# Runs of 32 in the loads of w1 and w2, zeros set by VectorE, and another order of the first rows, copies and fillers

## The chip, the cores and the metric

The kernel runs on 1 core of one Trainium2 chip. The metric is the device time of one launch in microseconds. Before the change it was 1922.45 us (median of three runs, 1921.44 to 1922.81).

## The reference

Inputs: x (8 batches of 1024 rows of 128), proj_q and proj_o (8 heads of 128x128), proj_k and proj_v (128x128), w1 (8 experts, 128x512), w2 (8 experts, 512x128), all float32. In short:

```python
xn = layernorm(x)                                   # over the last 128
Q = einsum('bnd,hdk->bhnk', xn, proj_q); K = xn @ proj_k; V = xn @ proj_v
weights = softmax(einsum('bhnk,bmk->bhnm', Q, K))
Y = einsum('bhnv,hdv->bnd', einsum('bhnm,bmv->bhnv', weights, V), proj_o)
mid = einsum('amh,ehn->aemn', xn, w1)
out = x + Y + einsum('aemn,enh->amh', mid, w2)
```

Keys and values are shared by the heads, and there is no nonlinearity between w1 and w2.

## The kernel before

**What is computed.** Per head the query and key projections are multiplied into one matrix (`wqk_product`), and the value and output projections into another (`wvo_product`), so that the logits are (xn wqk) xn^T. w1 and w2 are multiplied and summed over experts and hidden units into a single 128x128 matrix `wf` (`ffn_weights`). A unit u is one batch and head, 64 in all. A row i is one block of 128 queries against all 1024 keys, 8 to a unit and 512 in all. The product of weights and values uses a scheme with seven products instead of eight (`product`, with sums and differences of blocks made by GpSimd in `sum_early` and `sums_late`, and of values at the end of `values`).

**A row.** `logits(i)` is two halves of matmuls (`logits_half`, eight 512-wide matmuls together: each float32 product is two instructions, for two halves of the array). `exponents(i)` takes the row maximum on VectorE (`nmax`) and the exponential on ScalarE, which also gives the row's sum. `divide(i)` takes the reciprocal on VectorE (`rinv`) and multiplies on ScalarE. `weights_t(i - 1)` turns the weights of the row before in blocks of 32x32 on VectorE, and after each fourth row `move_blocks` moves the blocks between partitions with 16 DMAs on SyncE's queue (SP), which completes the transposition. Twelve rows later (`LAG`) the products of the unit follow, `PAIRS` of them to a row; a pair is four 512-wide matmuls. The last four rows use `LAST_PAIRS`, and turn their weights on TensorE (`weights_t_pe`).

**What sets the order.** It is written out by hand: each engine runs its instructions in the order of the program text. Two PSUM buffers (tag `sc`) serve the logits in turn, so the logits of row i wait until the exponents of row i-2 (or, with a large query product between, of row i-1) have been read. Four more banks (`bank`, tags `acc0` to `acc3`) serve the small products of the start in turn. A bank is free when its copy to SBUF is done.

**The start.** SP loads x's first batch in four pieces, then the projections, w1, w2 and the next batch's rows. Statistics (`stats_pair`), normalization (`norm_pair`) and transposition (`xn_t_pair`) go by pairs of 128-row chunks. `keep_clock` puts filler matmuls on zeros (`idle`, written to PSUM tile `pidle`) between them; GpSimd sets the zeros. Then the table `early` names which preparations go behind the logits of which row: the other wqk products, the queries, the transposes of proj_o (`wo_part`), the wvo products, the first values and the ffn products. `W1` names the rows after which VectorE turns a quarter of w1.

**w1 and w2.** w1 is held as `w1s`, two halves of four experts. Hidden units are spread over partitions so that 32x32 turns on VectorE bring them onto partitions. Before, a half is one DMA in which a partition receives 8 KB in one piece, and both sides of the turn (`turn_w1`, L224) step through memory in strides (16 elements read, 4 written). w2 has a partition order to match.

Of the kernel before, what the change touches and what calls it, by code (L numbers as in the profile page):

```python
# [9 lines left out]
F32 = mybir.dt.float32  # L10
AF = mybir.ActivationFunctionType
ALU = mybir.AluOpType
AX = mybir.AxisListType
# [4 lines left out]
def kernel(  # L18
# [76 lines left out]
    def slot(name):  # L95
        return ps_sc.tile([P, S], F32, tag="sc", name=name)
# [69 lines left out]


    for e in range(2):
        w1_e = w1[ts(e, NQ)].rearrange("r (j c) n -> (r j) (c n)", c=NQ)
        nc.sync.dma_start(w1s[:, e].rearrange("p c n -> p (c n)"), w1_e)  # L170
    for e in range(2):
        w2_e = w2[ts(e, NQ)].rearrange("r (q b) h -> (r q) b h", q=Q)
        nc.sync.dma_start(w2s[e], w2_e)
    load_rows(1)

    idle = late.tile([P, GS], F32, tag="diff", name="idle")
    nc.gpsimd.memset(idle, 0.0)
    ident = const.tile([P, P], F32, tag="ident", name="ident")
    make_identity(nc, ident)
    eps = const.tile([P, 1], F32, tag="eps", name="eps")  # L180
# [40 lines left out]
    def turn_w1(k):  # L221

        e, half = divmod(k, 2)
        nc.vector.transpose(  # L224
            w1T[:, ts(k, NB)].rearrange("p b (j c) -> p c b j", c=NQ),
            w1s[:, e].rearrange("p c (q b) -> p c b q", q=Q)[:, :, ts(half, NB)],
        )

    def ffn_weights(k):
# [57 lines left out]
    def xn_t_pair(k, copy):  # L287

        if k == 0:
            xnTs[0] = batch.tile([P, S], F32, tag="xnT", name="xnT_0")  # L290
        pt = bank(f"pxn_0_{k}")
        for c in range(2):
            nc.tensor.transpose(pt[:, ts(c, P)], xns[0][:, 2 * k + c, :], ident)
        copy(xnTs[0][:, ts(k, 2 * P)], pt[:, : 2 * P])

    def queries(u, first=0, last=S, copy=nc.scalar.copy):
        b, h = divmod(u, H)
        if first == 0:
            qTs[u] = work.tile([P, S], F32, tag="qT", name=f"qT_{u}")
        n = last - first  # L300
        pq = slot(f"pq_{u}") if n == S else bank(f"pq_{u}_{first}")
        for c in range(0, n, GS):
            w = min(GS, n - c)
            both_halves(pq[:, c : c + w], wqk[:, h, :], xnTs[b][:, first + c : first + c + w])
        copy(qTs[u][:, first:last], pq[:, :n])  # L305

    def values(s, c, copy=nc.scalar.copy):

        b, k = divmod(s, 2)
        if c == 0:  # L310
            vfs[s] = batch.tile([P, GN, 7, HC, HP], F32, tag="vf", name=f"vf_{s}")
        vf = vfs[s]
        if s == 0:
            pv = [bank(f"pv_{s}_{c}_{g}") for g in range(2)]
        else:
            both = slot(f"pv_{s}_{c}")
            pv = [both[:, ts(g, GS)] for g in range(2)]
        for g in range(2):
            both_halves(pv[g], xnTs[b][:, ts(c + g * HC, P)], wvo[:, ts(k, GN), :])
        v1, v2 = (t.rearrange("p (h j x) -> p h j x", h=GN, j=2) for t in pv)  # L320
        b11, b21, b22, t4, t1, t2, t3 = (vf[:, :, f, c] for f in range(7))
        b12 = t1
        nc.scalar.copy(vf[:, :, 0:5:4, c], v1)  # L323
        copy(vf[:, :, 1:3, c], v2)
        nc.gpsimd.tensor_sub(t3, b22, b12)  # L325
        nc.gpsimd.tensor_sub(t1, b12, b11)  # L326
        nc.gpsimd.tensor_sub(t2, b22, t1)
        nc.gpsimd.tensor_sub(t4, b21, t2)

# [4 lines left out]
    def logits_half(i, g):  # L336
        u, n = divmod(i, NB)
        if g == 0:
            pls[i] = slot(f"pl_{i}")
        both_halves(  # L340
            pls[i][:, ts(g, GS)], qTs[u][:, ts(n, P)], xnTs[u // H][:, ts(g, GS)]
        )

    def exponents(i):
        pl = pls.pop(i)
        nmax = small.tile([P, 1], F32, tag="nmax", name=f"nmax_{i}")
        nc.vector.reduce_max(nmax, pl, AX.X, negate=True)  # L347
        sums[i] = small.tile([P, 1], F32, tag="sums", name=f"sums_{i}")
        if i == NS - GN:
            spare.append(scratch("vf", VF, batch))  # L350
        if i < NS - GN:
            es[i] = work.tile([P, S], F32, tag="e", name=f"e_{i}")
        else:
            es[i] = spare[0][:, ts(i + GN - NS, S)]
        nc.scalar.activation(es[i], pl, AF.Exp, bias=nmax, accum_out=sums[i])  # L355

    def logits(i):
        logits_half(i, 0)
        logits_half(i, 1)
        exponents(i)  # L360

    def divide(i):
# [288 lines left out]
    def copy_wqv(first, last, copy):  # L651
        copy(wqvT[:, first:last], pwqs.pop(first)[:, : last - first])
# [6 lines left out]
    def keep_clock(*widths):  # L659

        for n in widths:
            nc.tensor.matmul(
                pidle[:, :n], lhsT=idle[:, :P], rhs=idle[:, :n], start=True, stop=True
            )
# [4 lines left out]
    def stats_pair(k):  # L669
        row_stats(x_0, 0, (2 * k, 2 * k + 1))  # L670

    pidle = slot("pidle")
    xns[0] = rows_tile("xn_0")
    keep_clock(GS)
    stats_pair(0)
    transposed(wkqT, [wk, wqv[:, 0]], "pwk", nc.scalar.copy)
    keep_clock(P, P, P)
    stats_pair(1)
    wqk_product(0, 1)
    keep_clock(P, P)  # L680
    norm_pair(0)
    xn_t_pair(0, nc.scalar.copy)
    keep_clock(P)
    norm_pair(1)
    xn_t_pair(1, nc.scalar.copy)
    stats_pair(2)
    queries(0, 0, P)
    stats_pair(3)
    queries(0, P, GS)
    logits_half(0, 0)  # L690
    turn_wqv(1, 5)
    norm_pair(2)
# [2 lines left out]
    xn_t_pair(3, nc.vector.tensor_copy)  # L695
    copy_wqv(1, 5, nc.scalar.copy)
    turn_wqv(5, 9)
    copy_wqv(5, 9, nc.vector.tensor_copy)
    logits_half(0, 1)
    exponents(0)  # L700

    def on_vector(task, *args):
        return lambda: task(*args, nc.vector.tensor_copy)

    early = {
        1: [on_vector(wqk_product, 1, 3), lambda: queries(0, GS, S)],
        2: [on_vector(wqk_product, 4, 4), lambda: queries(1, 0, GS)],
        3: [
            on_vector(wo_part, 0),
            lambda: wo_part(1, nc.scalar.copy),  # L710
            lambda: queries(1, GS, S),
        ],
        4: [lambda: wvo_product(0), on_vector(wvo_product, 1)],
        5: [on_vector(values, 0, 0)],
        6: [on_vector(values, 0, 1)],
        7: [on_vector(values, 0, 2)],
        9: [lambda: values(0, 3)],
        10: [lambda: ffn_weights(0), lambda: ffn_weights(1)],
        11: [lambda: ffn_weights(2), lambda: ffn_weights(3)],
    }  # L720
    W1 = {0: [0], 9: [1], 10: [2, 3]}

    PAIRS = (2, 2, 1, 2)
    LAST_PAIRS = (2, 1, 1, 1)
    COLLECT = {0: [0], 2: [1], 3: [2, 3], 4: [4], 6: [5], 7: [6, 7, 8], 8: [9], 10: [10], 11: [11]}

    FIRST_ROWS = 4
# [20 lines left out]

    for i in range(NS):
        m = i % GN  # L750
        if i > 0:
            logits(i)
        for task in early.get(i, ()):
            task()
        if 0 <= i - 1 < NS - GN:
            weights_t(i - 1)
        divide(i)
        for k in W1.get(i, ()):
            turn_w1(k)


        v, n = divmod(i - LAG, NB)
        if n == 6 and v + 1 >= 0:
            sum_early(v + 1)


        if i >= LAG:
            run((PAIRS if i < NS - GN else LAST_PAIRS)[m] + (n == 0 and v % H == H // 2 + 1) * 2)
            if n == 0:
                sums_late(v, nc.gpsimd)  # L770
        if i % NB == 0 and i > 0 and i // NB + 1 < B * H:
            queries(i // NB + 1)
        if i % NB == GN and i >= LAG:
            s, r = divmod(i + 20, 32)
            if s < 2 * B:
                values(s, r // NB)


        if i == 8:
            load_x(0)  # L780
        if i == NS // B:
            ones_of_last_rows()
        for b in range(1, B):
            r = i - FIRST_ROWS if b == 1 else i - (b - 2) * H * NB - 44
            if r in ROWS:
                ROWS[r](b)
            r = i - 20 if b == 1 else i - (b - 1) * H * NB
            if r in (0, 4, 8, 12):
                if r == 0:
                    turn_rows(b)  # L790
                move_rows(b, r // 4)
        b, r = divmod(i - 23, H * NB)
        if r == 0 and b < B:
            row_diff(b)


        b, r = divmod(i - 69, H * NB)
        if 0 <= b:
            for n in COLLECT.get(r, ()):
                collect(b, n)  # L800
            if r in (15, 19, 23, 27):
                if r == 15:
                    turn_out(b)
                move_out(b, (r - 15) // 4)
            elif r == 36:
                finish(b)
            elif r == 39:
                store(b)
            elif r == 43:
                load_x(b + 1)  # L810
# [1 line left out]
    sum_early(B * H - 1)  # L812
    weights_t_pe(NS - 4)
    weights_t_pe(NS - 3)
    run(3)
    weights_t_pe(NS - 2)
    weights_t_pe(NS - 1)
    for j in range(2):
# [39 lines left out]
```

## Time and profile before

| | |
|---|---|
| median of three runs | 1922.45 us |
| the profiled execution | 1922.09 us, of which the span of instructions is 1920.0 us |
| TensorE (PE) busy | 1910.9 us |
| VectorE (DVE) busy | 1405.5 us |
| GpSimd (POOL) busy | 1406.6 us |
| ScalarE (ACT) busy | 1352.9 us |
| granted TensorE clock | 1.000 |
| first matmul of a product with the weights (L448) | 58.74 us |

The page of the profile counts busy time by engine, and the timeline lists instructions by their start. Matmuls are pipelined: the busy time given for a group of them reaches past the start of the next group. PEld is TensorE's loading of weights, SPq the DMA issue queue of SyncE. L103 is the line of a helper, so that the tile's name tells the matmuls apart: `pl` logits, `pq` queries, `pv` values, `pwqk` and `pwvo` products of projections, `pwf` products of w1 and w2, `pxn` transposes of rows, `pe` transposes of the last weights.

### The profile page before, as it was taken

How to read it: one execution, taken by the hardware profiler on the slowest of the kernel's cores; microseconds unless marked ns; L12 is line 12 of the kernel's file. 1: busy time of each engine (PE TensorE's matmuls, PEld its weight loads, DVE VectorE, ACT ScalarE, POOL GpSimd, SP SyncE). 2: the span in 40 equal slices, each digit the busy share in tenths (PEclk: the TensorE clock that was granted, in tenths of full speed). 3: DMA queues.
4: the chain of work that ended last, by engine and by line, in shares of the span. 5: the costliest groups of instructions: out<-in, count | busy, mean ns of one | idle time of the engine just before them, and what ended most of it. 6: DMA issues, size and time to landing. Idle time of an engine off the chain costs nothing.

```text
span 1920.0 us, 26851 instructions
## 1 busy us (share of the span) xinstructions
PE 1910.9 (100%) x9026; PEld 649.2 (34%) x9026; DVE 1405.5 (73%) x1783; ACT 1352.9 (70%) x1818; POOL 1406.6 (73%) x593
## 2 busy tenths in 40 slices
PE   9999999999999999999999999999999999999998
PEld 4433333333333333333333333333333333333333
DVE  7777778767786777777777777776778776777775
ACT  7677777777776777777777777777677766777764
POOL 2877777688676886777967778768687777677764
PEclk9999999999999999999999999999999999999999
DMA  6676676676766766677667676676767667567673
GB/s 196 145 158 145 143 155 155 148 166 148 161 144 153 172 152 144 151 159 166 143 152 158 152 172 138 155 156 146 183 139 153 148 155 171 132 141 157 153 163 90
DMA packets 140137, 293.49 MB, mean 153 GB/s; under 512 B 40928, under 2 KB 74464, under 8 KB 139488
## 3 DMA queue, kind: packets, MB, share of 16 engines
q1 hardware_dynamic: 139168, 291.39, 67.5%
q8 instruction: 72, 1.18, 0.3%
q14 instruction: 65, 0.53, 0.1%
q10 hardware_dynamic: 832, 0.39, 0.1%
HBM read 13.76 MB, written 4.19 MB: 9 GB/s over the span
## 4 chain that ended last, share of the span: by engine, by line
PE 76%; POOL 10%; SPq 5%; DVE 3%; ACT 2%; DMA 2%; issue 1%; POOLq 0%; ACTq 0%; DVEq 0%
PE pl L103 36%; PE acc L448 31%; SPq L403 5%; PE pv L103 4%; PE pq L103 4%; POOL f L426 3%; POOL g L423 3%; POOL g L424 3%; DVE nmax L347 2%; DMA g<-turned 1%; ACT e L355 1%; DVE turned L387 1%; PE acc L481 1%; ACT e L365 1%; POOL vf L326 0%
## 5 line engine op out<-in xcount | busy, mean ns | idle before, releaser
L103 PE MATMUL pl<-xnT,qT 128*64 128x512 f32 x4096 | 966.5, 592 | 1.4 <-ACT e L355 0.9
L347 DVE TENSOR_REDUCE nmax<-pl 128x1 f32<-128x1024 f32 x512 | 626.4, 1224 | 405.3 <-PE pl L103 404.6
L448 PE MATMUL acc<-g,vf 128*64 128x512 f32 x2560 | 852.2, 592 | 0.0
L355 ACT ACTIVATE e<-pl,nmax 128x1024 f32<-128x1024 f32 x508 | 565.7, 1114 | 406.1 <-DVE nmax L347 406.1
L365 ACT ACTIVATE e<-e,rinv 128x1024 f32<-128x1024 f32 x508 | 583.4, 1148 | 117.8 <-DVE rinv L364 117.6
L387 DVE STREAM_TRANSPOSE turned<-e 128x1024 f32<-128x1024 f32 x508 | 628.8, 1238 | 10.3
L103 PEld LDWEIGHTS pl<-xnT,qT 128*64 128x64 f32 x4096 | 292.9, 137 | 587.6 <-issue 536.5
L448 PE MATMUL acc<-f,vf 128*64 128x512 f32 x1016 | 487.0, 592 | 0.0
L423 POOL TENSOR_TENSOR g<-g,g 128x2048 f32<-128x2048 f32 x63 | 287.0, 4556 | 267.1 <-DMA g<-turned 135.4
L448 PEld LDWEIGHTS acc<-g,vf 128*64 128x64 f32 x2560 | 250.4, 137 | 510.8 <-issue 507.1
L418 POOL TENSOR_TENSOR f<-g 128x2048 f32<-128x2048 f32 x63 | 287.1, 4557 | 168.2 <-PE acc L448 87.0
L426 POOL TENSOR_TENSOR f<-g,g 128x2048 f32<-128x2048 f32 x63 | 287.4, 4562 | 4.9
L424 POOL TENSOR_TENSOR g<-f,g 128x2048 f32<-128x2048 f32 x63 | 286.9, 4554 | 0.3 <-PE acc L448 0.3
L448 PEld LDWEIGHTS acc<-f,vf 128*64 128x64 f32 x1016 | 139.2, 137 | 0.0
L103 PE MATMUL pq<-xnT,wqk 128*64 128x512 f32 (+1 forms) x516 | 121.5, 590 | 0.5 <-DVE wqk L214 0.5
L103 PE MATMUL pv<-wvo,xnT 128*64 128x512 f32 x512 | 120.8, 592 | 0.0
L364 DVE RECIPROCAL rinv<-sums 128x1 f32<-128x1 f32 x512 | 83.9, 164 | 47.8 <-ACT scratch_vf L355 4.0
L355 ACT ACTIVATION_READ_ACCUMULATOR e<-pl,nmax 128x1 f32 x508 | 97.4, 192 | 0.0
L325 POOL TENSOR_TENSOR vf<-vf 128x256 f32<-128x256 f32 x64 | 46.9, 732 | 36.2 <-ACT vf L323 30.9
L305 ACT COPY qT<-pq 128x1024 f32<-128x1024 f32 (+2 forms) x67 | 64.0, 955 | 0.0
L103 PEld LDWEIGHTS pv<-wvo,xnT 128*64 128x64 f32 x512 | 36.7, 137 | 73.5 <-issue 69.7
L103 PEld LDWEIGHTS pq<-xnT,wqk 128*64 128x64 f32 x516 | 36.7, 137 | 72.2 <-issue 70.7
(107 smaller groups left out, 545.1 us busy)
## 6 DMA issues: line engine op xcount, KB each, us to landing
g<-turned SPq DMA_DIRECT2D x2032, 128.0 KB, 2.4
xn<-in_L_attn_x_dram SPq DMA_DIRECT2D x7, 512.0 KB, 4.7
xnT<-xnt SPq DMA_DIRECT2D x112, 32.0 KB, 1.9
out<-yt SPq DMA_DIRECT2D x112, 32.0 KB, 1.9
x<-in_L_attn_x_dram SPq DMA_DIRECT2D x6, 512.0 KB, 4.3
out_dram<-x SPq DMA_DIRECT2D x6, 512.0 KB, 5.4
scratch_g<-in_L_ffn_w_dram SPq DMA_DIRECT2D x2, 1024.0 KB, 8.3
scratch_f<-in_L_ffn_w_dram SPq DMA_DIRECT2D x2, 1024.0 KB, 12.0
```

The lines of the kernel that those rows point to most:

```text
L103: nc.tensor.matmul(dst[r], lhsT=lhsT[:, r], rhs=rhs, start=start, stop=stop)
L347: nc.vector.reduce_max(nmax, pl, AX.X, negate=True)
L355: nc.scalar.activation(es[i], pl, AF.Exp, bias=nmax, accum_out=sums[i])
L364: nc.vector.reciprocal(rinv, sums.pop(i))
L365: nc.scalar.mul(es[i], es[i], rinv)
L387: nc.vector.transpose(turned[k].rearrange("p k c t q -> p c k t q")[:, :, :, j, :], es.pop(i).rearrange("p (c k q) -> p c k q", k=NQ, q=Q),)
L403: nc.sync.dma_start(dst[ts(d, Q), r], src[ts(r, Q), d])
L418: nc.gpsimd.tensor_add(f1s[u], key_half(g0s[u], 0), key_half(g0s[u], 1))
L423: engine.tensor_sub(x1, y1, x1)
L424: engine.tensor_sub(x2, f1s[u], y1)
L426: engine.tensor_sub(f4s[u], y2, x2)
L448: nc.tensor.matmul(accs[b, acc][ts(half, HP)], lhsT=vfs[u // GN][:, u % GN, f, c, :], rhs=w[:, :, c, :], start=(h == 0 and c == first), st ...
```

## The change

- w1: eight DMAs instead of two. Piece c of a half gives each partition 2 KB, one expert's row among 32 consecutive ones, and the source runs over 4 experts, 32 rows and 512 columns. A turn then reads and writes runs of 32 elements.
- w2: eight DMAs instead of two, one an expert, in which each of 32 partitions receives 16 pieces of 512 bytes.
- VectorE sets the zeros of the fillers. There is one 128-wide filler more ahead of the first transposes, and two fewer around the first row transposes.
- In the first rows the row maximum is an instruction of its own step (`row_max`), and the logits of row 1 go ahead of the loop. The copies of products go to ScalarE, or are deferred (`defer`) and flushed to VectorE behind the reciprocal of the row. The table of preparations, the turns of w1 and the last rows' pairs are spread otherwise.

```diff
     for e in range(2):
-        w1_e = w1[ts(e, NQ)].rearrange("r (j c) n -> (r j) (c n)", c=NQ)
-        nc.sync.dma_start(w1s[:, e].rearrange("p c n -> p (c n)"), w1_e)
+        for c in range(NQ):
+            w1_c = w1[ts(e, NQ)].rearrange("r (c j) n -> c r j n", c=NQ)[c]
+            nc.sync.dma_start(w1s[:, e, c], w1_c)
     for e in range(2):
-        w2_e = w2[ts(e, NQ)].rearrange("r (q b) h -> (r q) b h", q=Q)
-        nc.sync.dma_start(w2s[e], w2_e)
+        for r in range(NQ):
+            w2_r = w2[e * NQ + r].rearrange("(b q) h -> q b h", q=Q)
+            nc.sync.dma_start(w2s[e][ts(r, Q)], w2_r)
...
-    nc.gpsimd.memset(idle, 0.0)
+    nc.vector.memset(idle, 0.0)
...
         nc.vector.transpose(
-            w1T[:, ts(k, NB)].rearrange("p b (j c) -> p c b j", c=NQ),
-            w1s[:, e].rearrange("p c (q b) -> p c b q", q=Q)[:, :, ts(half, NB)],
+            w1T[:, ts(k, NB)].rearrange("p b (c j) -> p c b j", c=NQ),
+            w1s[:, e].rearrange("p c (b q) -> p c b q", q=Q)[:, :, ts(half, NB)],
         )
...
-        nc.gpsimd.tensor_sub(t3, b22, b12)
-        nc.gpsimd.tensor_sub(t1, b12, b11)
-        nc.gpsimd.tensor_sub(t2, b22, t1)
-        nc.gpsimd.tensor_sub(t4, b21, t2)
+        def differences(copy):
+            nc.gpsimd.tensor_sub(t3, b22, b12)
+            nc.gpsimd.tensor_sub(t1, b12, b11)
+            nc.gpsimd.tensor_sub(t2, b22, t1)
+            nc.gpsimd.tensor_sub(t4, b21, t2)
+        deferred.append(differences)
+        if copy != defer:
+            flush(copy)
...
+    nmaxs = {}
+    def row_max(i):
+        nmaxs[i] = small.tile([P, 1], F32, tag="nmax", name=f"nmax_{i}")
+        nc.vector.reduce_max(nmaxs[i], pls[i], AX.X, negate=True)
     def exponents(i):
-        pl = pls.pop(i)
-        nmax = small.tile([P, 1], F32, tag="nmax", name=f"nmax_{i}")
-        nc.vector.reduce_max(nmax, pl, AX.X, negate=True)
+        pl, nmax = pls.pop(i), nmaxs.pop(i)
...
         logits_half(i, 1)
+        row_max(i)
         exponents(i)
...
+    deferred = []
+    def defer(dst, src):
+        deferred.append(lambda copy: copy(dst, src))
+    def flush(copy):
+        while deferred:
+            deferred.pop(0)(copy)
...
-    keep_clock(GS)
+    keep_clock(GS, P)
     stats_pair(0)
     transposed(wkqT, [wk, wqv[:, 0]], "pwk", nc.scalar.copy)
     keep_clock(P, P, P)
     stats_pair(1)
     wqk_product(0, 1)
-    keep_clock(P, P)
+    keep_clock(P)
     norm_pair(0)
     xn_t_pair(0, nc.scalar.copy)
-    keep_clock(P)
     norm_pair(1)
     xn_t_pair(1, nc.scalar.copy)
+    queries(0, 0, P)
     stats_pair(2)
-    queries(0, 0, P)
+    queries(0, P, GS, defer)
     stats_pair(3)
-    queries(0, P, GS)
+    flush(nc.scalar.copy)
     logits_half(0, 0)
     turn_wqv(1, 5)
...
     turn_wqv(5, 9)
-    copy_wqv(5, 9, nc.vector.tensor_copy)
+    copy_wqv(5, 9, nc.scalar.copy)
     logits_half(0, 1)
+    row_max(0)
     exponents(0)
-
-    def on_vector(task, *args):
-        return lambda: task(*args, nc.vector.tensor_copy)
+    logits_half(1, 0)
+    logits_half(1, 1)
+    row_max(1)
     early = {
-        1: [on_vector(wqk_product, 1, 3), lambda: queries(0, GS, S)],
-        2: [on_vector(wqk_product, 4, 4), lambda: queries(1, 0, GS)],
-        3: [
-            on_vector(wo_part, 0),
-            lambda: wo_part(1, nc.scalar.copy),
-            lambda: queries(1, GS, S),
-        ],
-        4: [lambda: wvo_product(0), on_vector(wvo_product, 1)],
-        5: [on_vector(values, 0, 0)],
-        6: [on_vector(values, 0, 1)],
-        7: [on_vector(values, 0, 2)],
-        9: [lambda: values(0, 3)],
-        10: [lambda: ffn_weights(0), lambda: ffn_weights(1)],
+        0: [lambda: wqk_product(1, 3)],
+        1: [lambda: queries(0, GS, S), lambda: wqk_product(4, 4)],
+        2: [lambda: queries(1, 0, GS)],
+        3: [lambda: wo_part(0, defer), lambda: wo_part(1, defer), lambda: queries(1, GS, S)],
+        4: [lambda: wvo_product(0), lambda: wvo_product(1, defer)],
+        5: [lambda: values(0, 0, defer)],
+        6: [lambda: values(0, 1, defer)],
+        7: [lambda: values(0, 2, defer)],
+        8: [lambda: values(0, 3)],
+        9: [lambda: ffn_weights(0)],
+        10: [lambda: ffn_weights(1)],
         11: [lambda: ffn_weights(2), lambda: ffn_weights(3)],
     }
-    W1 = {0: [0], 9: [1], 10: [2, 3]}
+    W1 = {0: [0], 8: [1], 9: [2], 10: [3]}
     PAIRS = (2, 2, 1, 2)
-    LAST_PAIRS = (2, 1, 1, 1)
+    LAST_PAIRS = (2, 1, 1, 2)
...
     for i in range(NS):
-        if i > 0:
+        if i == 1:
+            exponents(1)
+        elif i > 1:
             logits(i)
         for task in early.get(i, ()):
             task()
         if 0 <= i - 1 < NS - GN:
             weights_t(i - 1)
         divide(i)
+        flush(nc.vector.tensor_copy)
         for k in W1.get(i, ()):
             turn_w1(k)
...
     weights_t_pe(NS - 3)
-    run(3)
+    run(2)
```

## The prediction

> **What bounds the kernel now.** I read the page first, then TensorE's waits in two stretches (0 to 60 us, and the rest), then its timeline in order of time up to 60 us, then the groups, the DMAs and the last 40 us.
>
> ```profile
> span 1920.0 us, 26851 instructions
> PE 1910.9 (100%) x9026; PEld 649.2 (34%) x9026; DVE 1405.5 (73%) x1783; ACT 1352.9 (70%) x1818; POOL 1406.6 (73%) x593
> ```
>
> TensorE (PE) is busy for all but 9.1 us. No other engine is above 73%, so the change can win only where PE stands still, or by taking work from PE. The waits up to 60 us (engine, line, releaser, us in total, times, longest), and then the only one after it:
>
> ```profile
> PE pidle L662 <- POOL idle L177: 1.3, 1, 1.3
> PE pl L103 <- ACT e L355: 0.9, 1, 0.9
> PE pq L103 <- DVE wqk L214: 0.5, 1, 0.5
> PE pwf L103 <- DVE scratch_vf L224: 0.4, 1, 0.4
> ```
>
> ```profile
> PE pe L376 <- ACT scratch_vf L355: 0.7, 1, 0.7
> ```
>
> 1,800 us between them are without a wait. Everything lies in the first 57 us and the last 32. Now PE's timeline (start, busy, line, what, count):
>
> ```profile
> 17.19 1.07 PE L103 MATMUL pwqk<-scratch_turned 128*64 128x128 f32 x16
> 18.78 1.08 PE L103 MATMUL pq<-xnT,wqk 128*64 128x512 f32 x4 [0.52 <-DVE wqk L214]
> ...
> 26.87 1.89 PE L103 MATMUL pl<-xnT,qT 128*64 128x512 f32 x8
> 28.81 1.94 PE L103 MATMUL pv<-wvo,xnT 128*64 128x512 f32 x8
> ...
> 39.16 1.89 PE L103 MATMUL pq<-xnT,wqk 128*64 128x512 f32 x8
> 41.96 1.94 PE L103 MATMUL pl<-xnT,qT 128*64 128x512 f32 x8 [0.91 <-ACT e L355]
> ...
> 45.44 1.89 PE L103 MATMUL pl<-xnT,qT 128*64 128x512 f32 x8
> 47.42 3.71 PE L103 MATMUL pwf<-scratch_f,scratch_vf 128*64 128x128 f32 x64
> 50.97 1.89 PE L103 MATMUL pl<-xnT,qT 128*64 128x512 f32 x8
> 53.28 3.91 PE L103 MATMUL pwf<-scratch_f,scratch_vf 128*64 128x128 f32 x64 [0.43 <-DVE scratch_vf L224]
> 57.02 1.89 PE L103 MATMUL pl<-xnT,qT 128*64 128x512 f32 x8
> ```
>
> Busy times overlap, so I read starts. Undisturbed, the next group follows eight 512-wide matmuls after 1.715 us (34.01, 35.72, 37.44 and 39.16 are such starts), and 128-wide ones cost 0.0536 each (x16 0.86, x64 3.43). What is over is lost: before 18.78 18.78-17.19-0.86 = 0.73; before 28.81 0.23; before 41.96 1.09; before 47.42 0.26; before 53.28 53.28-50.97-1.715 = 0.60; before 57.02 0.31. Together 3.22 us, more than the waits list shows.
>
> **The change part by part.**
>
> *The start.* The chain of waits runs on PE from 3.70 to 10.77, fillers included. Fillers: one 128-wide goes ahead of the first transposes; one of two ahead of the first row transpose goes, and the one between the two row transposes goes. Their prices from starts: 0.85/2 = 0.43 (four matmuls from 5.83 to 6.68) and 0.22 (6.94 to 7.16), 0.65 in all. The added one costs nothing: it follows the 512-wide one, which starts at 1.31, and the second weight transpose waits for its DMA until 3.70; the copy that reads it stands behind two rstd instructions on ScalarE until 4.83, a cover of 0.3. The zeros' memset took 0.52 on GpSimd; no VectorE memset is in the trace, its nearest row is a 128x512 copy from PSUM, 0.69: so the fillers start between 0.3 earlier and 0.2 later, and only fillers feel it. The full 0.65 does not arrive. ScalarE's rstd for rows 256 to 511 now stands behind the first query copy (0.25), so norm_pair(2) starts at about 8.58, not 8.42; four normalizes (1.19), the last transposes and the copy follow as now (10.37 to 11.36 is 0.99): 8.58+1.25+0.99 = 10.82 for the second logits half, not 11.36. Gain 0.5 (bounds 0.1 and 0.65).
>
> *The wait of 0.73* is for the copy of wqk heads 1 to 3 on VectorE, behind a 1.22 row maximum. That product is now issued one row earlier and copied on ScalarE right after the first exponents, at about 14.4; its reader comes at about 17.5. Gone. Covered: ScalarE's new load. From the first exponents at 13.2 (10.82+0.86 matmul+0.26 latency+1.22 maximum) it does exponents 0, copy 0.4, multiply 0, exponents 1, two copies, multiply 1, exponents 2: 3x1.2+0.4+2x0.47+2x1.05 = 7.0, done at 20.3. PE reaches the logits that need this bank after 0.86+3x1.715+0.64+0.86+3x0.86+0.86 = 10.9, at 21.8. Cover 1.5.
>
> *wo copies* (two, deferred to VectorE behind the reciprocal of row 3): exponents 3 end 20.3+0.47+1.05+1.2 = 23.0, reciprocal 0.2, copy 0.7: 23.9, while PE is free for wvo at 21.8+1.7 = 23.5. A new wait: 0.3 to 0.4; I take 0.3, bounds 0 and 0.7 (a whole copy).
>
> *The 0.23* (wvo's copy behind exponents 4): exponents now run about 1.5 us ahead; gone, with 0.1 of cover. *The 1.09*: logits 9 wait for exponents 8, which need 0.26+1.22+1.2 = 2.7 after logits 8, while only 1.715 of queries lie between. values(0,3) moves there, 1.715 more: 3.43 against 2.7. Gone. *The 0.26* was that move's other end, the ffn product right behind values' copies. Gone.
>
> *The turns of w1* and the 0.91 us of the ffn products.
>
> ```profile
> L224 DVE STREAM_TRANSPOSE scratch_vf<-scratch_g 128x1024 f32<-128x1024 f32 x4 | 8.5, 2158 | 0.0
> ```
>
> ```profile
> L387 DVE STREAM_TRANSPOSE turned<-e 128x1024 f32<-128x1024 f32 x508 | 628.8, 1238 | 10.3
> ```
>
> Same size, but the second reads and writes runs of 32 and takes 1.24, not 2.16. The new w1 layout makes the first like it: 0.92 off each. With that, and turns and products one row apart instead of in pairs (turns 2 and 3 stood from 51.09 to 55.17), 0.60 and 0.31 go.
>
> *Copies deferred behind the reciprocals, GpSimd's subtractions with them:* VectorE has 3.24 us per row here against PE's 3.43, in either order; GpSimd waits 30 us for its first subtraction. Nothing.
>
> *The loads.* Sixteen DMAs for four. SP issued x in four at 0.5 each, so the row load behind them issues some 6 to 10 us later than 7.77; it landed 14.5 after, and its reader comes at 42. SP's next work is at 28.96. Nothing, if the data lands as now:
>
> ```profile
> GB/s 0 167 205 256 313 339 408 415 431 426 415 421 335 152 11 0 0 0 0 0 175 221 205 210 208 205 186 0 46 216 210 85 202 213 208 197 215 175 3 0
> ...
> scratch_g<-in_L_ffn_w_dram SPq DMA_DIRECT2D x2, 1024.0 KB, 8.3
> ```
>
> In slices of 1.5 us, the loads run at some 420 GB/s, 2.5 us for 1 MB; the first half of w1, behind wo (landed 3.92+6.0 = 9.9), lands at 12.4. VectorE wants it at about 14.9 (the first turn), with some 0.6 to spare behind it: free up to 15.5, and from there each us late is a us of PE. In the trace's semaphore records each of these loads lands in sixteen steps; no load here has an outer dimension under 32. From these rows I take no loss; the other bound is the second rival's.
>
> The Trainium skill ("DMA: Bandwidth & Descriptors", "Why a DMA increments its semaphore by 16 and not by 1") speaks against this: a DMA is split over the largest number of engines, up to 16, that divides the slowest dimension of both sides. The new w1 source runs over r = 4 first, which would leave 4 of 16 engines, and by that an estimate of 19 to 20 us for the first half and a total of about 1922. No row here shows such a load.
>
> *The end.* One pair (4 matmuls, 0.857) moves ahead of the last transposes.
>
> ```profile
> 1888.90 1.11 ACT L355 ACTIVATE scratch_vf<-pl,nmax 128x1024 f32<-128x1024 f32 x1
> ...
> 1890.15 1.09 PE L376 MATMUL pe<-ident,scratch_vf 128*128 128x128 f32 x8 [0.69 <-ACT scratch_vf L355]
> ```
>
> The second transposes wait for the last exponents to free their bank; PE is idle from 1889.24 to 1890.15. The pair needs only blocks that had landed, and fills this. Next late: products at 1894.95 whose blocks landed at 1894.9. Gain 0.8 (0.7 to 0.9).
>
> *Sum:* 0.5+3.22-0.3+0.8 = 4.2. The profiled run took 1922.09 (span 1920.0 and 2.09 around it), 0.36 under the median of 1922.45; the same 4.2 off the median gives 1918.2. With the bounds and the runs' spread (1921.44 to 1922.81): 1917.0 to 1920.0.
>
> **The rivals.** *First rows give nothing* (ScalarE's copies cost what the order gains; only 1.17 at the ffn products, half of the 1.09 and 0.8 at the end remain): 2.5 saved, 1919.8. Against it: the cover of 1.5.
>
> *The first half of w1 lands late.* The change then doesn't do what it says: the turn is shorter but waits. Bound: each 256 KB piece takes what a 1 MB load took, 2.5. From 9.2 to 9.9 on, four pieces end at 19.2 to 19.9, 3.7 to 4.4 of stall on VectorE, against 4.2: 1921.7 to 1922.6, nothing seen. For it: the piece's other shape. Against: the full rate in every slice.
>
> *The same wait, slower than before:* it decides from a landing at 19.7, and costs over 0.2% from 23.5, that is 3.4 us a piece. At 25 the time is 1918.2+9.5 = 1927.7. Then VectorE stands from 14.9, exponents 2 follow, and PE stops at 21.8.
>
> **How the numbers follow.** 0.2% (3.84 us, below 1918.6) is about what a measurement of this kernel can tell from no change. Forecast 0.64, of which 0.46 beyond 0.2% and 0.18 within; late but even 0.17, nothing from the first rows 0.05, both within; slower 0.14. So faster 0.46, same 0.40, slower 0.14. The range 1917.0 to 1924.4 takes in the even cases and leaves out the slower one and a little below.
>
> **What would show it.** Right: no PE wait from pq on wqk, from pl on e near 40, from pwf on the turns; turns at 1.24; the transposes at the end without a 0.7 wait; DVE's first turn following the reciprocal at once. Wrong: DVE idle before the first turn, released by a DMA, and PE idle near 22; a w1 landing beyond 15.5; a PE wait on woT above 0.7; a first logits half later than 8.7.

## The result, and the profile after

The changed kernel takes 1928.88 us (median of six runs, 1927.76 to 1929.96), against 1921.68 us for the kernel before on the same chip (six runs, 1921.44 to 1922.81). The ratio is 1.0036 with an interval of [1.0023, 1.0049]: slower by some 7 us, where the forecast was 4.2 faster, and outside the range. The profiled execution took 1927.87 us with a span of 1926.1, 6.1 longer than the span before.

TensorE's waits up to 70 us, in the same view as before (engine, line, releaser, us in total, times, longest):

```profile
PE pwf L103 <- DVE scratch_vf L226: 4.2, 1, 4.2
PE pl L103 <- ACT e L367: 2.1, 1, 2.1
PE pidle L675 <- DVE idle L179: 1.5, 1, 1.5
```

After 70 us the view lists none. So the four small waits of before (0.9, 0.5, 0.4 and the 0.7 at the end) are gone, as forecast, and two larger ones are there. TensorE's timeline (start, busy, line, what, count, idle before) shows what they cost:

```profile
21.93 1.08 PE L103 MATMUL pq<-xnT,wqk 128*64 128x512 f32 x4
25.16 3.53 PE L103 MATMUL pl<-xnT,qT 128*64 128x512 f32 x8 [2.14 <-ACT e L367]
28.68 1.94 PE L103 MATMUL pwvo<-scratch_vf,scratch_turned 128*64 128x512 f32 x8
...
52.80 1.92 PE L103 MATMUL pl<-xnT,qT 128*64 128x512 f32 x8
58.95 5.66 PE L103 MATMUL pwf<-scratch_f,scratch_vf 128*64 128x128 f32 x64 [4.23 <-DVE scratch_vf L226]
64.43 1.89 PE L103 MATMUL pl<-xnT,qT 128*64 128x512 f32 x8
66.15 1.89 PE L461 MATMUL acc<-g,vf 128*64 128x512 f32 x8
```

The first product with the weights starts at 66.15 instead of 58.74: 7.4 us are lost by then, and 0.85 of it is won at the end. Two stops carry the loss. Beside the wait, the matmuls behind each stop are slow: the eight logits matmuls from 25.16 to 28.68 take 3.52 instead of 1.715. VectorE's timeline shows where the stops come from:

```profile
15.48 0.15 DVE L377 RECIPROCAL rinv<-sums 128x1 f32<-128x1 f32 x1
20.32 1.25 DVE L226 STREAM_TRANSPOSE scratch_vf<-scratch_g 128x1024 f32<-128x1024 f32 x1 [4.69 <-DMA scratch_g<-in_L_ffn_w_dram]
...
48.86 0.29 DVE L246 BATCH_NORM_STATS2 st<-xn 128x6 f32<-128x128 f32 x1 [2.39 <-DMA xn<-in_L_attn_x_dram]
...
56.46 1.25 DVE L400 STREAM_TRANSPOSE turned<-e 128x1024 f32<-128x1024 f32 x1 [5.19 <-DMA g<-turned]
...
57.67 1.22 DVE L226 STREAM_TRANSPOSE scratch_vf<-scratch_g 128x1024 f32<-128x1024 f32 x1
```

Each of VectorE's three new waits is for a DMA: for the first half of w1, for the next batch's rows, and for the moves of the weights' blocks (`g<-turned`), which must be done before the buffer `turned` is written again. The turn itself went from 2.16 to 1.25. SP's queue and the DMA rate of the first 60 us (slices of 1.5 us):

```profile
4.35 14.87 SPq L171 DMA_DIRECT2D scratch_g<-in_L_ffn_w_dram  x8
19.27 18.66 SPq L175 DMA_DIRECT2D scratch_f<-in_L_ffn_w_dram  x8
37.98 1.85 SPq L125 DMA_DIRECT2D xn<-in_L_attn_x_dram  x1
39.95 25.94 SPq L416 DMA_DIRECT2D g<-turned  x32
```

```profile
GB/s 0 181 244 237 310 186 99 98 101 98 109 102 98 100 100 216 161 85 98 119 178 151 60 170 199 201 151 192 166 203 234 168 80 183 199 213 199 199 219 199
```

Before, SP's queue was:

```profile
4.39 2.39 SPq L170 DMA_DIRECT2D scratch_g<-in_L_ffn_w_dram  x2
6.83 0.90 SPq L173 DMA_DIRECT2D scratch_f<-in_L_ffn_w_dram  x2
28.96 24.01 SPq L403 DMA_DIRECT2D g<-turned  x32
```

SP was through w1 and w2 at 7.7 and sent the first blocks at 28.96; now it sends them at 39.95. From 9 to 18 us, where some 420 GB/s were moved before, it is 100, and stays so to 22 us. The semaphore records say why: each piece of w1 lands in four steps (the loads before in sixteen), and its last steps come at 12.28, 14.92, 17.56 and 20.20 for the first half, 2.64 us a piece of 256 KB, that is 99 GB/s. The windows view (its last two columns are the mean busy share of the 16 DMA engines and GB/s) agrees: a share of 0.26 is about four of sixteen, where it was 1.02 before (9 to 18 us).

```profile
9.00:12.00 3.00, 2.83 (x22) 1.56 (x18) 1.54 (x5) 2.02 (x6) 0.00 (x0) 1.00 0.26 98
12.00:15.00 3.00, 3.00 (x26) 1.65 (x24) 1.89 (x2) 1.18 (x4) 0.00 (x0) 1.00 0.26 100
```

The semaphore records also show how it goes on: of w2's first DMA twelve steps land by 25.28 and the last four from 34.14 to 35.54, so the engines that carry w1's pieces are some ten microseconds behind the others. SP issues no faster than these four engines work: from the fifth piece of w1 on, an issue lasts 2.5 us and ends 0.7 to 1.0 before the piece four ahead of it has landed, and w2's eight issues last from 1.0 to 6.1. What an issue waits for inside, the records don't say. It isn't its semaphore, one of eight that these DMAs use in turn: the DMA that used it last had landed (at 7.47, for the issue from 11.60 to 14.11). So SP stands, with everything queued on it.

### The profile page after: what moved, and what is told of

The parts are those of the page before. It is cut to its first block, busy times and chain, and to the rows that moved or that the text cites. A ratio compares the mean times of both kernels' runs of the same rounds, so it can differ in the third digit from the quotient of the medians.

```text
span 1926.1 us, 26863 instructions
## 1 busy us (share of the span) xinstructions
PE 1913.5 (99%) x9024; PEld 652.8 (34%) x9024; DVE 1401.5 (73%) x1782; ACT 1353.4 (70%) x1820; POOL 1406.2 (73%) x592
## 4 chain that ended last, share of the span: by engine, by line
PE 89%; DVE 3%; SPq 2%; ACT 2%; POOL 2%; DMA 1%; issue 0%; DVEq 0%; POOLq 0%
PE pl L103 41%; PE acc L461 37%; PE pq L103 5%; PE pv L103 5%; DVE nmax L356 2%; ACT e L367 1%; SPq L175 1%; SPq L171 1%; PE acc L494 1%; DMA g<-turned 1%; DVE turned L400 1%; ACT e L378 1%; DMA xn<-in_L_attn_x_dram 1%; SPq L416 1%; POOL f L439 0%; POOL g L436 0%
```

## The experiments

The first four were told in advance with three theories. A: a piece whose source runs over four experts first is carried by 4 of 16 DMA engines, and what lands late stops TensorE. B: it is the number of DMAs and their small runs that cost. C: the new order costs. The times of the kernel before beside each were 1921.75 to 1922.05.

**w1 one expert to a DMA.** The destination is the same; a DMA now fills 32 partitions, and its source runs over 32 rows first.

```diff
-            w1_c = w1[ts(e, NQ)].rearrange("r (c j) n -> c r j n", c=NQ)[c]
-            nc.sync.dma_start(w1s[:, e, c], w1_c)
+            w1_r = w1[e * NQ + r].rearrange("(c j) n -> j c n", c=NQ)
+            nc.sync.dma_start(w1s[ts(r, Q), e], w1_r)
```

> The changed kernel with w1 still in eight DMAs of 256 KB and the same place in memory for every element, but one DMA an expert: the source runs over 32 rows first, then 4 pieces of 2 KB, instead of 4 experts first. Theory A (a w1 piece whose source runs over 4 experts first lands in 4 steps and so uses 4 of 16 DMA engines; the late data is all that is wrong): first half of w1 landed by about 13 us, no wait of VectorE before the first turn, no wait of more than 1 us on TensorE after 12 us, the transposes at the end without a wait; 1917.5 to 1919. Theory B (the number of DMAs is what costs: each waits for the one eight before it, and runs of 2 KB and 512 bytes are slow): the first half still lands after 16 us, the row load after 40; 1924 or more. Theory C (the order of the first rows costs): no DMA wait, but 1922 or more.

Measured: 1916.94 (1916.5 to 1918.7), ratio 0.9975 [0.9966, 0.9984]. This is faster than both kernels. The DMAs are as many and their runs as short as in the changed kernel, so B falls; the order is the same, so C falls. The pieces land in sixteen steps, the first half by 14.82, just ahead of the turn at 14.94 (later than I expected). TensorE's timeline has no stop:

```profile
22.22 1.89 PE L103 MATMUL pl<-xnT,qT 128*64 128x512 f32 x8
23.98 1.94 PE L103 MATMUL pwvo<-scratch_vf,scratch_turned 128*64 128x512 f32 x8
...
49.81 3.69 PE L103 MATMUL pwf<-scratch_f,scratch_vf 128*64 128x128 f32 x64
53.30 1.91 PE L103 MATMUL pl<-xnT,qT 128*64 128x512 f32 x8
55.02 1.92 PE L461 MATMUL acc<-g,vf 128*64 128x512 f32 x8
```

SP's queue in the same kernel:

```profile
4.45 6.07 SPq L171 DMA_DIRECT2D scratch_g<-in_L_ffn_w_dram  x8
11.27 12.87 SPq L175 DMA_DIRECT2D scratch_f<-in_L_ffn_w_dram  x8
24.18 1.25 SPq L125 DMA_DIRECT2D xn<-in_L_attn_x_dram  x1
26.73 24.64 SPq L416 DMA_DIRECT2D g<-turned  x32
```

The loads are not as fast as before (about 210 GB/s), but SP is through the row load at 25.4 and sends the first blocks at 26.73, when they are turned. The difference between this kernel and the changed one, 66.15-55.02 = 11.13 us up to the first product, is all in three places: 0.62 at the very start (the full clock came at 7.93 in one profile and at 6.20 in the other; that it is the cause is not shown), (28.68-21.93)-(23.98-21.31) = 4.08 at the first stop, and (64.43-52.80)-(53.30-48.09) = 6.42 at the second; 21.31 and 48.09 are the same two groups' starts here.

**The order alone.** The changed kernel with the loads and the turn sides of before.

```diff
-        for c in range(NQ):
-            w1_c = w1[ts(e, NQ)].rearrange("r (c j) n -> c r j n", c=NQ)[c]
-            nc.sync.dma_start(w1s[:, e, c], w1_c)
+        w1_e = w1[ts(e, NQ)].rearrange("r (j c) n -> (r j) (c n)", c=NQ)
+        nc.sync.dma_start(w1s[:, e].rearrange("p c n -> p (c n)"), w1_e)
...
```

> The changed kernel with the loads of w1 and w2 and the sides of the turn as before; order, zeros, copies, fillers and end as changed. Theories A and B: turns of 2.16 us, no wait for a DMA, and between 1918.5 and 1920, since the turns cost 0.9 more each than in the run by expert. Theory C: 1922 or more.

Measured: 1919.08 (1918.55 to 1920.01), ratio 0.9986 [0.9977, 0.9995]. The order, with the zeros, the fillers and the pair at the end, wins 2.7 by itself; one wait on a turn is left:

```profile
PE pwf L103 <- DVE scratch_vf L224: 1.2, 1, 1.2
```

The 2.1 from here to the kernel with w1 by expert is what the turn in runs of 32 is worth, less what its slower loads cost; the two were not told apart.

**The loads alone.** The kernel before with the loads and turn sides of the change, and its own order.

```diff
-        w1_e = w1[ts(e, NQ)].rearrange("r (j c) n -> (r j) (c n)", c=NQ)
-        nc.sync.dma_start(w1s[:, e].rearrange("p c n -> p (c n)"), w1_e)
+        for c in range(NQ):
+            w1_c = w1[ts(e, NQ)].rearrange("r (c j) n -> c r j n", c=NQ)[c]
+            nc.sync.dma_start(w1s[:, e, c], w1_c)
...
```

> The kernel before with only the loads of w1 and w2 and the sides of the turn as changed. Theory A: the first turn waits from about 15 to 20 us as in the changed kernel, but here the row maximum and the copy of wqk stand behind it, so TensorE stops at about 18 us for 5 us; then the row load and the moved blocks come late, a second stop of some 5 us, each with the clock at half for 3.4 us behind it: 8 to 13 us slower than before. Theory B: the same. Theory C: within 2 us of before, as the order is unchanged.

Measured: 1933.94 (1933.63 to 1934.19), ratio 1.0063 [1.0050, 1.0075]. The loads cost 12.2 in the old order, inside the 8 to 13 that theories A and B gave. TensorE waits 4.4 for a turn, 3.0 for the copy of wqk behind the first turn, and 1.3 for values.

**The first turn in row 7 instead of row 0.** The changed kernel with all turns in rows 7 to 10.

```diff
-    W1 = {0: [0], 8: [1], 9: [2], 10: [3]}
+    W1 = {7: [0], 8: [1], 9: [2], 10: [3]}
```

> The changed kernel with the first turn of w1 in row 7 instead of row 0 (its reader comes in row 9). The data of the first half lands at 20 us, so nothing waits for it. Theory A with two stops that add up: 4 us faster than the changed kernel (the first stop of 2.4 and the slow clock behind it, 1.8), about 1924.5. Theory A with the second stop at a time that the DMA queue fixes (VectorE gets its block buffer back at 56.5 us, whenever it comes there): the second stop gets longer by what the first one loses, 8 us instead of 4.4 on TensorE, and the time stays at 1927.5 to 1929.5.

Measured: 1928.47 (1927.76 to 1929.32), ratio 1.0034 [1.0022, 1.0047], the same as the changed kernel. The waits moved:

```profile
PE pl L103 <- ACT e L367: 4.2, 1, 4.2
PE pwf L103 <- DVE scratch_vf L226: 2.7, 1, 2.7
```

The first stop is gone and its time is lost at the second (this `pl` is at 52.87, and the first product with the weights at 67.30). So what ends last in this kernel is not the first half of w1, but what stands behind w2 on SP, and moving the turn doesn't help.

**The pair at the end alone.** The kernel before with only this:

```diff
-    LAST_PAIRS = (2, 1, 1, 1)
+    LAST_PAIRS = (2, 1, 1, 2)
...
-    run(3)
+    run(2)
```

> The kernel before, with one edit: LAST_PAIRS is (2, 1, 1, 2), so that the fourth pair of products goes ahead of the last two rows' transposes. Theory of the prediction: 0.8 us less than before (0.7 to 0.9), about 1920.9; TensorE's wait of 0.7 us on the last exponents is gone, and the 16 transposes run in one go. Rival (the time comes back at the products behind, whose blocks land later): as before, 1921.7, with a new wait at the last products.

Measured: 1921.19 (1920.28 to 1922.12), ratio 0.9996 [0.9987, 1.0005]; the time alone can't tell 0.6 from nothing. The trace can: from the last four rows' final logits to the last 16 transposes it was 1893.90-1885.70 = 8.20, and is 1892.38-1885.04 = 7.34, 0.86 less. The 0.7 wait is gone and no wait takes its place, and the products behind keep their distance.

**Only the first half of w1 in the changed form**, the second by expert.

```diff
             if e == 0:
                 w1_c = w1[ts(e, NQ)].rearrange("r (c j) n -> c r j n", c=NQ)[c]
                 nc.sync.dma_start(w1s[:, e, c], w1_c)
+            else:
+                w1_r = w1[e * NQ + c].rearrange("(c j) n -> j c n", c=NQ)
+                nc.sync.dma_start(w1s[ts(c, Q), e], w1_r)
```

> The changed kernel, with the second half of w1 loaded one expert to a DMA (as in the experiment that loads both halves so), and the first half in the changed form. Theory A with a price on both stops: the first half still lands at about 20.2, the first stop stays (2.4 us of waits and 1.8 us of half clock), the second goes if SP is through w2 by about 30 us: 1916.9+4.2, about 1921 (1920.5 to 1922). Rival (only the second stop costs anything, the first is caught up): about 1917. Rival (the second stop stays, as SP's queue was already too late): about 1927.

Measured: 1926.55 (1926.13 to 1928.13), ratio 1.0025 [1.0015, 1.0035], 5.5 us more than I expected. The DMAs behind share the slow four engines (the second half's first DMA has twelve steps landed by 14.46 and the last four from 24.60 to 25.89): the first half's pieces land at 11.83, 17.73, 22.07 and 24.70, 4.5 later than in the changed kernel. The first stop grows and the second is gone:

```profile
PE pl L103 <- ACT e L371: 7.7, 1, 7.7
```

VectorE waits 10.2 for the first half here, and the stretch from the queries to wvo's product is 33.18-20.91-2.67 = 9.60 too long (2.67 is 23.98-21.31, the same stretch with w1 by expert), which is the whole difference of the two times. In the changed kernel the wait and the stretch were 4.7 and 4.1 too long. Both say the same: 0.6 of a late landing is covered, and every further us is one of TensorE.

**Only the second half in the changed form**, the first by expert (the same diff with `e == 1`).

> The changed kernel, with the first half of w1 loaded one expert to a DMA and the second half in the changed form. Theory A: no first stop; the second half lands by about 26, w2 and the row load some 10 us later than with both halves by expert, and SP's next blocks too. If SP is through w2 by about 32 us, no second stop: 1917 to 1918. If it is not, a second stop of 2 to 4 us with a slow clock: 1920 to 1923. Rival (the two stops are one chain, both from the first half): 1917 in any case.

Measured: 1922.86 (1922.03 to 1924.58), ratio 1.0007 [0.9998, 1.0016]: 5.9 more than with both halves by expert. All of w1 is there in time (first half by 14.84, second by 28.70), yet the second stop is there, because SP reaches the row load at 32.46 and the blocks only then. VectorE's wait:

```profile
DVE turned L404 <- DMA g<-turned: 5.2, 1, 5.2
```

**w2's DMAs from ScalarE's queue.** The kernel above, with w2 issued in rows 3 to 8 by ScalarE, so that SP is not held.

```diff
+    def load_w2(k):
+        e, r = divmod(k, NQ)
+        w2_r = w2[k].rearrange("(b q) h -> q b h", q=Q)
+        nc.scalar.dma_start(w2s[e][ts(r, Q)], w2_r)
...
         flush(nc.vector.tensor_copy)
+        for k in {3: [0], 4: [1], 5: [2], 6: [3], 7: [4, 5], 8: [6, 7]}.get(i, ()):
+            load_w2(k)
```

> The kernel with the first half of w1 by expert and the second half in the changed form (1922.9), with one more edit: w2's eight DMAs are issued by ScalarE in rows 3 to 8 instead of by SP. Theory (the second stop comes from SP's queue: the blocks of the weights stand behind w2's issues, which wait for the slow pieces of w1): SP is through the row load by some 15 us, the first blocks go out when they are turned (near 27), no second stop: 1917 to 1918.5. Rival (the four engines that carry the pieces are behind, and the blocks wait for them on any queue): second stop as before, about 1923. Rival (w2 then lands too late, or its issues hold ScalarE): a wait of the ffn products on w2 or of logits on exponents, 1919 to 1922.

Measured: 1919.62 (1918.46 to 1921.3), ratio 0.9989 [0.998, 0.9997]. SP's queue and what is left of TensorE's waits:

```profile
13.37 3.12 SPq L125 DMA_DIRECT2D xn<-in_L_attn_x_dram  x1
27.00 27.54 SPq L421 DMA_DIRECT2D g<-turned  x32
```

```profile
PE pl L103 <- ACT qT L312: 1.9, 1, 1.9
```

The blocks go out at 27.00 and no ffn product waits for a turn: the second stop was SP's queue. This run moves w2's bytes to later too, so by itself it doesn't tell a held queue from busy engines. The changed kernel's own times do: its blocks go out 13.2 later than with w1 by expert (39.95 against 26.73), and the sixteenth DMA of them lands some 15 later (VectorE starts on its landing at 56.46; there it is at 41.48), so at most 1.8 of it is on the way. Of the 2.7 that remain above 1916.94, 1.9 is the price of the third theory: ScalarE is held for 2.6 us at the issues of w2's last two DMAs, and the copy of the queries behind them is late.

**Fillers in the second stop.** The changed kernel, with five 512-wide matmuls on zeros ahead of the third ffn product.

```diff
-        11: [lambda: ffn_weights(2), lambda: ffn_weights(3)],
+        11: [lambda: fill(5), lambda: ffn_weights(2), lambda: ffn_weights(3)],
```

> The changed kernel, with five 512-wide fillers on zeros (4 x 0.2125 us each at full clock, 4.25 us in all, against a wait of 4.4) put into TensorE's second stop, ahead of the third ffn product. Theory: the half clock after a stop comes from the standstill, and the fillers prevent it: the wait of 4.2 on the turn falls to some 0.2, the 64 matmuls of that product take 3.43 and not 5.48, and 2.0 of the time goes: 1926.9. Rival (the clock falls for another reason, such as the DMA traffic, or five fillers are no cover): the 5.48 stays, 1928.9 or a little more.

Measured: 1928.1 (1927.55 to 1929.54), ratio 1.0035 [1.0022, 1.0049]: no gain that can be told, where I expected 2.0. The half clock did go:

```profile
59.55 1.97 PE L103 MATMUL pwf<-scratch_f,scratch_vf 128*64 128x128 f32 x32
62.36 1.97 PE L103 MATMUL pwf<-scratch_f,scratch_vf 128*64 128x128 f32 x32 [0.85 <-DVE scratch_vf L226]
64.16 1.89 PE L103 MATMUL pl<-xnT,qT 128*64 128x512 f32 x8
```

Now the fourth product waits for its turn. VectorE's late turn of the weights is at:

```profile
56.19 1.25 DVE L400 STREAM_TRANSPOSE turned<-e 128x1024 f32<-128x1024 f32 x1 [5.48 <-DMA g<-turned]
```

From this turn to the next logits behind the ffn products it is 64.43-56.46 = 7.97 in the changed kernel, at half clock, and 64.16-56.19 = 7.97 here, at full clock. The same holds at the first stop, where this run also kept its full clock: from the first turn to wvo's product 28.68-20.32 = 8.36 and 29.09-20.73 = 8.36. VectorE's chain sets both ends; the slow matmuls lay beside it and cost nothing here. My first reading of the trace, 2.4 of wait and 1.8 of clock, was wrong in its second part.

**The fillers and zeros of before**, in the kernel with w1 by expert.

```diff
-    nc.vector.memset(idle, 0.0)
+    nc.gpsimd.memset(idle, 0.0)
...
-    keep_clock(GS, P)
+    keep_clock(GS)
...
-    keep_clock(P)
+    keep_clock(P, P)
...
+    keep_clock(P)
```

> The changed kernel with both halves of w1 loaded one expert to a DMA, and with the fillers and their zeros as before (one 512-wide filler ahead of the first transposes, three, two and one 128-wide ones after, zeros set by GpSimd). Theory of the prediction: the fillers that the change took out were worth 0.65, of which up to 0.5 arrives: 1917.2 to 1917.6 against 1916.9. Rival (the fillers lay in waits, and the clock comes up by them): 1916.9 or less.

Measured: 1917.75 (1916.81 to 1918.78), ratio 0.9979 [0.997, 0.9987], 0.8 more than with the new fillers. The sign is as forecast; the intervals of the two overlap, and the first logits half moves by more than that between profiles (below). So a gain of the new fillers is not shown.

**The old order with w1 by expert.** The kernel before with the loads and turn of the first experiment.

> The kernel before, with only the loads and the turn of the change, and w1 one expert to a DMA (its order of rows, copies and fillers as before). Theory of the prediction: turns at 1.25 instead of 2.16, and the 0.60 and 0.31 at the ffn products go: 1921.7-0.9, about 1920.8. Rival (these loads are half as fast as the loads before, and the second pair of turns or the blocks come late): 1921.7 or more, with a wait of the ffn products or of the turns on a DMA.

Measured: 1920.37 (1919.07 to 1921.17), ratio 0.9991 [0.9982, 0.9999]: 1.7 less than before, where 0.9 was expected. Beside the waits on the turns (0.60 and 0.31) the 0.73 of the wqk copy is gone too: pwqk starts at 18.39 and the queries at 19.27, without a wait. That copy stood behind the first turn and the row maximum on VectorE, of which the prediction names only the second, and the shorter turn frees it. The 0.92 on the exponents stays, which only the new order removes.

## Why the prediction was wrong

**The step that failed** is in *The loads*: "From these rows I take no loss". It rested on a rate of 420 GB/s and sixteen steps of landing that were measured on loads of another shape, and the sentence ahead of it says so itself: no load there had an outer dimension under 32. The new source has one of 4. The Trainium skill ("DMA: Bandwidth & Descriptors", "Why a DMA increments its semaphore by 16 and not by 1") gave the number of engines as the largest that divides the slowest dimension of both sides; the runs agree (four steps a piece, 99 GB/s), and the estimate of 19 to 20 us that the prediction drew from it for the first half was nearly met, at 20.20. A rule that names the shape at hand should have weighed more than rows of another shape.

**The second step that failed** is in the same part: "SP's next work is at 28.96. Nothing, if the data lands as now", and with it the second and third rivals, which priced the late load at the first turn alone. The landing was theirs (19.2 to 19.9 forecast, 20.20 measured), and so was the price at that place: free to 15.5, then us for us, gives 4.7, and the stop was 4.08. But "1921.7 to 1922.6, nothing seen" left out the queue behind. SP's issues of w1 and w2 took 33.5 us instead of 3.3, and the blocks of the weights, due when SP stood at w2, came 11 us late. In the changed kernel this chain sets the time: with the first stop taken away (the late turn) the time is the same, and with SP freed the second stop is gone. So the rival's threshold for slower, a landing of 23.5, was wrong too: it was slower at 20.2. The first stop has a price of its own all the same: with only the first half in the changed form it is the one stop that is left, and costs 9.6.

**What was right** shows in the kernel with w1 by expert, which is closest to the change as I took it to be (its loads are slower, but in time). It is 4.8 us faster than before, for 4.2 forecast; by its own profile the span is 5.0 less, 58.74-55.02 = 3.72 up to the first product, 0.85 at the end, and 0.46 behind the last matmul group, which I can't attribute (from there to the end it is 5.96 before and with the pair alone, 5.50 and 5.48 in the changed kernel and here). The terms:

| term | forecast | measured |
|---|---|---|
| a turn | 1.24 | 1.25 |
| start, to the first logits half | 0.5 | 8.70-8.22 = 0.48 in these two profiles |
| waits up to the first product, less the new one | 3.22-0.3 | 3.72-0.48 = 3.24 |
| of it, new wait on the wo copies | 0.3 | 23.98-22.22-1.715 = 0.05 |
| the pair at the end | 0.8 | 0.85 |

The start agrees by luck: the second logits half follows the first by 2.66 in the kernel before, the changed one and the one by expert alike, so ScalarE's rstd did not stand in the way as I had worked out, and the first half itself moves with the clock. For fillers and zeros the trace has 0.14 later (1.45 against 1.31), inside the bounds. The term that was mis-sized here is the wait on the wo copies, 0.3 in the sum and 0.05 in the trace. Two sums in the rivals are slightly off as well: 2.5 saved gives 1919.9, not 1919.8, and a stall of 3.7 gives 1921.9, not 1921.7.

The prediction named the sign by which it would be wrong, "DVE idle before the first turn, released by a DMA, and PE idle near 22; a w1 landing beyond 15.5". All three are in the profile. So is a fourth, "a first logits half later than 8.7" (8.84), but the kernel by expert, which has the same start, has it at 8.22.

## What to carry to other kernels

When a load's shape changes, price it by the shape of its source's and destination's outermost dimension, not by the rate of the loads it replaces, and count the steps in which it lands. Then price its queue: list what stands behind it on the issuing engine and when each is due, since the buffer that stops the compute may have nothing to do with the data that is late. And before a slow stretch behind a stop is added to the price, ask which engine's chain reaches the end of it.

## What the runs showed of the hardware that I had not expected

**Loads into 32 partitions** (w1 by expert) land in sixteen steps, but a piece of 256 KB follows the other after 1.16 to 1.25 us, some 220 GB/s, half of what the loads into 128 partitions moved before (420). The engines are no less busy for it (a share of 1.08 from 9 to 18 us, against 1.02 before), and it is not the 2 KB pieces: in the DMA records a packet of 2 KB takes 159 ns on average here (10 to 14.5 us) and 86 ns in the changed kernel (10 to 20 us).

**The clock falls on a grid.** The windows view (us; busy us and count of PE, PEld, DVE, ACT, POOL; granted clock; DMA share; GB/s) of the changed kernel, and then of the one with fillers:

```profile
24.00:27.00 3.00, 1.84 (x6) 0.61 (x8) 2.76 (x4) 3.00 (x5) 0.00 (x0) 0.67 0.59 123
57.00:60.00 3.00, 1.05 (x12) 1.05 (x14) 3.00 (x5) 1.15 (x1) 3.00 (x1) 0.85 0.95 209
```

```profile
24.00:27.00 3.00, 1.43 (x8) 0.48 (x8) 2.74 (x4) 3.00 (x6) 0.00 (x0) 1.00 0.73 130
```

The clock records change only at whole multiples of 3.41 us from the moment the full clock came (in the changed kernel at 7.93, half from 24.99 to 28.41 and from 59.13 to 62.54). Where TensorE, counted by starts, stood for 2.2 or more of a step of that grid, the next was at half clock (2.2 in the changed kernel's first stop, 2.5 with only the second half changed); where it stood for 2.1 or less it was not (1.96 in the run with fillers, whose first stop of 3.2 lies across two steps; 2.1 with w2 from ScalarE). By the ends of matmuls that the profile models, the two sides almost touch: 1.98 in the changed kernel's first stop, 1.96 in the run with fillers. Once down, the clock can stay down: with the late turn it was half for four steps (51.03 to 64.68), the first three with 1.3 to 1.8 of standstill, and came back after one with none. The Trainium skill ("TensorE: Matmul & The Clock Gate", "Part 1: The HAM clock gate (the "warmup" mystery)") has the window of 3.4 us and says half clock comes after at least one idle window; these runs agree on the window, and show less than a whole idle one to be enough. What the limit is, they don't settle.

**When the full clock comes** differs between profiles, from 5.2 to 10.1 us, and the first logits half moves with it, from 7.8 to 10.2. These are profiles of thirteen kernels, one of each. The three latest (8.86, 9.34 and 10.11) have the old fillers and zeros, but so do two of 5.43 and 6.75; with the new ones it lies between 5.15 and 7.93. Whether the fillers have a part in it, these runs don't settle.
